# A planned two-level fast matmul kernel: sums assigned to fixed engines, a third p5 tile, zero matmuls at the start, and two products moved in the TensorE order

## Chip, cores and metric

The kernel runs on one core of one Trainium2 chip. The metric is the device time in microseconds (us); lower is better. Before the change three runs were taken, and their median is compared. Besides these, one execution was recorded by the hardware profiler; all durations of single instructions below come from that one.

## Reference

A batch of 1024 rows `x` with 512 features goes through a factorization layer with 64 embeddings:

```python
def _L0_rec_ref(x, weight, lin_w, lin_b):
    out_lin = x @ lin_w.T + lin_b
    xv = jnp.einsum('bf,efm->bem', x, weight)
    zp = jnp.einsum('bf,efm->bem', jnp.square(x), jnp.square(weight))
    interaction = 0.5 * jnp.sum(jnp.square(xv) - zp, axis=1)
    return out_lin + interaction
```

`x` is 1024 x 512, `weight` 64 x 512 x 512, `lin_w` 512 x 512, all in float32. There are three parts: `lin`, one matmul with a bias; `xv`, the large one, a 1024 x 512 by 512 x 32768 matmul whose result is only squared and summed over the embeddings; and `zp`, which needs just one small matmul, because the squared weights can be summed over the embeddings first.

## The kernel before, in words

**Tiling.** The columns of `weight` are cut into 16 groups of 2048 columns (32 output columns times 64 embeddings). For each group the kernel multiplies a 2 x 2 block matrix of x by a 2 x 2 block matrix of weights (`w11`, `w12`, `w21`, `w22`, 1 MB each) by a fast scheme with seven products in place of eight. It does so at two levels. Each of the seven outer products is called a *tree*; trees run in the order `ORDER = (1, 6, 2, 7, 5, 4, 3)`. Within a tree seven inner products are made, and `PLACE` gives each its place in the order of TensorE: product p of tree number s has the key `7 * s + PLACE[p]`. Products of up to three neighbouring trees alternate, so product 5 of a tree comes before the end of the tree before it. A product is two calls of matmul of 128 x 128 by 128 x 512 in float32, which the profile shows as four instructions. The trees are 3136 of the 3264 matmul instructions.

**Operands of a tree.** The x side (`X1` to `X7`) is made once at the start: two copies and sums of 1024 elements per partition on block level, then four sums of 256 elements per `X` (L280, and L372 for the form -a - b). The weight side is made for every tree: four sums `t1` to `t4` of 128 x 512 on GpSimd (L280), out of one weight tile, with two tiles for each. Trees 5 and 6 use `T1` and `T2`, sums of weight blocks that are built by a plain load (L309) and accumulating loads issued by GpSimd (L413). `w12` and `w21` get an accumulation of this kind later in the group.

**Results of a tree.** Products accumulate in PSUM banks `b1`, `b3` and the ring `b2`. `p5` and `p53` are copies of `b3` in SBUF, after product 5 and after product 3. Where the key word in the code is `early`, `p5` is a sum with an addend (`oa3` or `ob3`) made on VectorE; otherwise ScalarE copies it (L293). Outer results are kept in `oa0` to `oa3` and `ob0` to `ob3` and in the ring `c`. For tree 5 and the positions 1 and 3 the code does

```python
o = c_ring()
whole(p, b, p, psum=True)
whole(o, f"oa{pos}", p)
whole(f"ob{pos}", f"ob{pos}", p)
```

so `p` is read by two SBUF sums, `c` and `ob`. A finished result is squared on ScalarE (L295) and reduced on VectorE into `acc` (L302). Squares of the weights go the same way into `w2_sum`.

**Order of work.** Nothing is ordered by hand: each operation is given to a `Plan` with its cost on each engine that could do it, its reads and its writes. `Plan.order` works out the latest time of each from the TensorE chain, then simulates the engines and emits the instructions in the order that came out. Each engine, and each queue that issues transfers, then runs its own instructions strictly in that order. `HOP` is the time that the plan takes for a signal between engines. An operation with costs for VectorE and GpSimd could go to either. VectorE took one only when its latest time was under `spare` = 4 us away. For operations marked `both`, the plan also counted what the two engines lose when they run at once.

**Start and end.** Lin comes first: 64 matmul instructions (L331) on four banks, for which x and `lin_w` are loaded in quarters (k = 0 to 3) into `oa0` to `oa3`, `ob0`, `ob1`. Its bias is added on VectorE into `ob2`, `ob3`, `c_0`, `c_1`, and the sums are stored in DRAM (`lind`). At the end zp comes as 64 matmul instructions (L617) on the same banks, with x squared on VectorE beforehand (L588); the parts of `acc` are joined with lin (L598), zp is added (L280), and eight stores follow.

Of the kernel before, what the change touches and what calls it, by code (L numbers as in the profile page):

```python
# [11 lines left out]
F32 = mybir.dt.float32  # L12
# [4 lines left out]
P = 128  # L17
# [9 lines left out]
class Plan:  # L27
# [5 lines left out]

    HOP = 0.18

    def __init__(self):
        self.ops = []
# [19 lines left out]
        op.deps.discard(op.n)  # L59
        self.ops.append(op)  # L60

    def order(self, spare=4.0):
        ops = self.ops
        chain = sorted((o for o in ops if o.key is not None), key=lambda o: o.key)
        t = 0.0
        for o in chain:
            o.latest = t
            t += o.costs[PE]
        for o in reversed(ops):
            for d in o.deps:  # L70
                ops[d].succ.append(o.n)
        waiting = [len(o.succ) for o in ops]
        stack = [o for o in ops if not o.succ]
        while stack:
            o = stack.pop()
            latest = t if o.latest is None else o.latest
            cost = min(o.costs.values()) + o.land + self.HOP
            for x in o.succ:
                latest = min(latest, ops[x].latest - cost)
            o.latest = latest  # L80
            for d in o.deps:
                waiting[d] -= 1
                if not waiting[d]:
                    stack.append(ops[d])

        left = [len(o.deps) for o in ops]
        pending = {e: set() for e in (PE, ACT, DVE, POOL, SP)}
        free = dict.fromkeys(pending, 0.0)
        running = dict.fromkeys(pending)
        times = [self.HOP]  # L90
        done, late, nxt = [], 0.0, 0

        def release(o):
            for e in o.costs:
                pending[e].add(o.n)

        def ready(o):
            return max([0.0] + [ops[d].end for d in o.deps]) + self.HOP

        def longer(e, by):  # L100

            free[e] += by
            running[e].end += by
            heapq.heappush(times, free[e])
            heapq.heappush(times, running[e].end + self.HOP)

        for o in ops:
            if not left[o.n]:
                release(o)

        def pick(e, now):
            if e == PE:
                if nxt < len(chain):
                    o = chain[nxt]
                    if not left[o.n] and ready(o) <= now + 1e-6:
                        return o
                return None
            at = {n: ready(ops[n]) for n in pending[e]}
            for n in sorted((n for n in at if at[n] <= now + 1e-6),
                            key=lambda n: (ops[n].latest, n)):  # L120
                o = ops[n]
                if len(o.costs) > 1 and e == DVE and o.latest + late - now > spare:
                    continue
                until = now + o.costs[e]
                if not any(
                    now + 1e-6 < at[u] < until - 0.2
                    and ops[u].latest < o.latest
                    and ops[u].latest + late < until + 0.1
                    for u in at
                ):  # L130
                    return o
            return None

        while len(done) < len(ops):
            now = heapq.heappop(times)
            moved = True
            while moved:
                moved = False
                for e in pending:
                    if free[e] > now + 1e-6:  # L140
                        continue
                    o = pick(e, now)
                    if o is None:
                        continue
                    moved = True
                    if e == PE:
                        nxt += 1
                        late = max(late, now - o.latest)
                    cost = o.costs[e]

                    if e == DVE and o.both and free[POOL] > now + 0.1:
                        over = free[POOL] - now
                        cost += 0.9 * over
                        longer(POOL, 0.35 * over)
                    elif e == POOL and free[DVE] > now + 0.1 and running[DVE].both:
                        over = free[DVE] - now
                        cost += 0.5 * over
                        longer(DVE, 0.9 * over)
                    free[e] = now + cost
                    running[e] = o  # L160
                    o.end = free[e] + o.land
                    heapq.heappush(times, free[e])
                    heapq.heappush(times, o.end + self.HOP)
                    for f in o.costs:
                        pending[f].discard(o.n)
                    done.append((o, e))
                    for x in o.succ:
                        left[x] -= 1
                        if not left[x]:
                            release(ops[x])  # L170
        return done
# [3 lines left out]
def kernel(  # L175
# [34 lines left out]
    nc = tc.nc  # L210
# [43 lines left out]
        make(f"oa{pos}", half)  # L254
        make(f"ob{pos}", half)
    t_ring = {k: ring(f"t{k}", 2, [P, N]) for k in range(1, 5)}
    p5_ring, p53_ring = ring("p5", 2, half), ring("p53", 3, half)
    c_ring, wsq_ring = ring("c", 3, half), ring("wsq", 2, half)
    make("b1", [P, G, N], ps)
    make("b3", [P, G, N], ps)  # L260
    b2_ring = ring("b2", 2, [P, G, N], ps)
    acc_ring = ring("acc", 2, [P, NB, MG])
    w2_sum = sb.tile([P, NK, M], F32, tag="w2_sum", name="w2_sum")
    bias = sb.tile([P, M], F32, tag="bias", name="bias_sb")
    acc_dram = dram.tile([P, NB, M], F32, tag="accd", name="accd")
    lin_dram = dram.tile([P, NB, M], F32, tag="lind", name="lind")

# [1 line left out]
    engines = {DVE: nc.vector, POOL: nc.gpsimd}  # L269
    PAIR = 1.72  # L270

    def two_input(o, a, b, sub, size=1024, psum=False):

        costs = {DVE: 0.08 + 1.06 * size / 1024}
        if not psum:
            costs[POOL] = 0.14 + 2.19 * size / 1024

        def emit(e):
            f = engines[e].tensor_sub if sub else engines[e].tensor_add
            f(o, a, b)  # L280

        return costs, emit

    def whole(o, a, b, sub=False, only=None, psum=False):

        costs, emit = two_input(buf[o], buf[a], buf[b], sub, psum=psum)
        plan.add({e: c for e, c in costs.items() if only in (None, e)}, emit, (a, b), (o,),
                 both=not psum)

    def act(o, i, func, reads, writes, cost=1.04):  # L290
        def emit(_):
# [19 lines left out]

    x_src = xT.rearrange("(p k) b -> p k b", k=NK)
    lw_src = lin_wT.rearrange("(p k) m -> p k m", k=NK)
    nc.gpsimd.dma_start(bias, lin_b.partition_broadcast(P))
    for k in range(NK):
        q, r = divmod(k, KH)
        for h in range(2):
            name = f"oa{2 * h + q}"
            dma(buf[name][:, r, :], x_src[:, k, ts(h, H)], (), ((name, r),),
                1.2, 2.0, nc.sync if h == 0 else nc.scalar)  # L320
        dma(buf[f"ob{q}"][:, r, :], lw_src[:, k, :], (), ((f"ob{q}", r),), 1.2, 2.0)

    lin_banks = ["b1", "b3", "b2_0", "b2_1"]
    for k in range(NK):
        q, r = divmod(k, KH)
        for g, bank in enumerate(lin_banks):
            h = g // 2

            def emit(_, k=k, q=q, r=r, g=g, h=h, bank=bank):
                for j in range(G):  # L330
# [6 lines left out]
                    )  # L337

            plan.add({PE: PAIR}, emit, ((f"oa{2 * h + q}", r), (f"ob{q}", r)),
                     (bank,), key=-1000 + 4 * k + g)  # L340
    for g, bank in enumerate(lin_banks):
        o = ("ob2", "ob3", "c_0", "c_1")[g]
        for j in range(G):
            costs, emit = two_input(buf[o][:, j, :], buf[bank][:, j, :], bias, False, 512, True)
            plan.add(costs, emit, (bank,), ((o, j),))
        dma(lin_dram[:, ts(g, G), :], buf[o], ((o, 0), (o, 1)), (o,))

    def block4(i):
# [15 lines left out]
    def x_sum(i, o, a, b, kind, reads, size):  # L364

        if kind != "-a - b":
            costs, emit = two_input(o, a, b, kind == "a - b", size)
        else:
            costs = {DVE: two_input(o, a, b, True, size)[0][DVE]}

            def emit(_):
                nc.vector.scalar_tensor_tensor(o, a, -1.0, b, ALU.mult, ALU.subtract)  # L372
# [77 lines left out]
    def tree(s, g, i):  # L450
# [3 lines left out]
        for k, a, b, reads in (  # L454
# [2 lines left out]
            (3, b22, b12, (r,)),  # L457
            (4, b21, buf[t[2]], (r, t[2])),
        ):
            costs, emit = two_input(buf[t[k]], a, b, True, 512)  # L460
            plan.add({POOL: costs[POOL]}, emit, reads, (t[k],))
        rhs = {
            1: (b11, r), 2: (b21, r), 3: (b22, r), 4: (buf[t[4]], t[4]),
            5: (buf[t[1]], t[1]), 6: (buf[t[2]], t[2]), 7: (buf[t[3]], t[3]),
# [142 lines left out]
        add_acc(g, edge, M, buf[last][:, ts(g, G), :], reads)  # L607

    out_dst = out.rearrange("(n p) m -> p n m", p=P)
    w2_parts = tuple(("w2", row, m * MI) for row in range(2) for m in range(M // MI))  # L610
    for g, bank in enumerate(("b3", "b1", "b2_0", "b2_1")):
        o = acc_all[g]
        h = g // 2
        for j in range(G):
            def emit(_, bank=bank, g=g, h=h, j=j):
                for k in range(NK):
# [5 lines left out]
                    )  # L622

            plan.add({PE: 2 * PAIR}, emit, (xe[h, 0], xe[h, 1]) + w2_parts,
                     ((bank, j),) + ((bank,) if j == 0 else ()), key=1e6 + 2 * g + j)
            costs, emit = two_input(
                buf[o][:, j, :], buf[bank][:, j, :], buf[lin_all[g]][:, j, :], False, 512, True
            )
            plan.add(costs, emit, ((bank, j), lin_all[g], o), ((o, "out", j),))
            dma(out_dst[:, g * G + j, :], buf[o][:, j, :], ((o, "out", j),), ())  # L630
# [35 lines left out]
```

## Time and profile before

| | |
|---|---|
| device time, median of 3 | 1430.11 us (1429.66 to 1430.48) |
| device time of the profiled run | 1429.27 us |
| span of the profile, first to last instruction | 1427.5 us |
| TensorE matmul | 1409.1 us busy, 3264 instructions |
| VectorE | 1115.5 us busy, 946 instructions |
| GpSimd (POOL) | 1010.6 us busy, 703 instructions |
| ScalarE | 678.8 us busy, 692 instructions |
| moved by DMA | 200.96 MB, mean 141 GB/s; 269 GB/s in the first 10 us, 376 and 344 in the two after |

In the profile's lines, PE is TensorE's matmul and PEld its weight load, DVE is VectorE, ACT ScalarE, POOL GpSimd, SP the engine that issues most transfers. A timeline line gives start, duration (both in us), engine, line of the code, operation and operands (out<-in, the numbers of buffers left out), and in brackets the idle time just before and what ended it. Matmul ends are modelled, so the distance from one start to the next says more than the duration.

### The profile page before, as it was taken

How to read it: one execution, taken by the hardware profiler on the slowest of the kernel's cores; microseconds unless marked ns; L12 is line 12 of the kernel's file. 1: busy time of each engine (PE TensorE's matmuls, PEld its weight loads, DVE VectorE, ACT ScalarE, POOL GpSimd, SP SyncE). 2: the span in 40 equal slices, each digit the busy share in tenths (PEclk: the TensorE clock that was granted, in tenths of full speed). 3: DMA queues.
4: the chain of work that ended last, by engine and by line, in shares of the span. 5: the costliest groups of instructions: out<-in, count | busy, mean ns of one | idle time of the engine just before them, and what ended most of it. 6: DMA issues, size and time to landing. Idle time of an engine off the chain costs nothing.

```text
span 1427.5 us, 10368 instructions
## 1 busy us (share of the span) xinstructions
PE 1409.1 (99%) x3264; PEld 617.9 (43%) x3264; DVE 1115.5 (78%) x946; ACT 678.8 (48%) x692; POOL 1010.6 (71%) x703
## 2 busy tenths in 40 slices
PE   8999999999999999999999999999999999999998
PEld 3434444444444444444444444444444444444443
DVE  1779597886968779696877959788696978969785
ACT  1446354454635446364544635445463544636431
POOL 5886786857768686785958678685777868677660
PEclk9999999999999999999999999999999999999999
DMA  9656381745628175472836638274573817546331
GB/s 306 202 155 173 91 203 45 196 122 143 167 75 205 67 177 151 118 177 63 209 89 164 163 96 199 55 193 113 147 177 91 187 53 185 143 120 145 94 112 60
DMA packets 47286, 200.96 MB, mean 141 GB/s; under 512 B 19008, under 2 KB 20032, under 8 KB 24704
## 3 DMA queue, kind: packets, MB, share of 16 engines
q0 software_dynamic: 11600, 84.15, 30.2%
q1 hardware_dynamic: 35056, 115.09, 23.3%
q10 hardware_dynamic: 576, 1.05, 0.2%
q8 instruction: 27, 0.44, 0.1%
q14 instruction: 27, 0.22, 0.0%
HBM read 177.34 MB, written 6.16 MB: 129 GB/s over the span
## 4 chain that ended last, share of the span: by engine, by line
PE 92%; DMA 2%; POOL 2%; DVE 2%; issue 1%; ACT 0%; DVEq 0%; SPq 0%; ACTq 0%; POOLq 0%
PE b L472 90%; DMA T<-weight 2%; PE b L617 2%; DVE p L280 1%; POOL t L280 1%; POOL X L280 1%; DMA oa<-xT 0%; POOL ob L280 0%; DVE ob L280 0%; ACT X L293 0%; SPq L309 0%; POOL w L413 0%; DVE w22a L280 0%; DVEq L662 0%; ACTq L309 0%
## 5 line engine op out<-in xcount | busy, mean ns | idle before, releaser
L472 PE MATMUL b<-t,X 128*128 128x512 f32 x1792 | 806.1, 592 | 1.7 <-DVE ob L280 1.4
L472 PEld LDWEIGHTS b<-t,X 128*128 128x128 f32 x1792 | 339.2, 190 | 432.1 <-issue 419.9
L472 PE MATMUL b<-w,X 128*128 128x512 f32 x768 | 358.5, 592 | 3.4 <-DVE p L280 2.3
L280 POOL TENSOR_TENSOR t<-w 128x512 f32<-128x512 f32 x128 | 163.2, 1278 | 147.5 <-PE b L472 84.5
L472 PEld LDWEIGHTS b<-w,X 128*128 128x128 f32 x768 | 145.7, 190 | 187.8 <-issue 175.1
L293 ACT COPY p<-b 128x1024 f32<-128x1024 f32 x160 | 160.4, 1002 | 133.6 <-PE b L472 133.6
L295 ACT ACTIVATE oa<-oa 128x1024 f32<-128x1024 f32 x128 | 133.6, 1056 | 166.8 <-DVE oa L280 166.8
L280 POOL TENSOR_TENSOR t<-w,t 128x512 f32<-128x512 f32 x128 | 164.9, 1289 | 57.5 <-PE b L472 57.3
L472 PE MATMUL b<-T,X 128*128 128x512 f32 x384 | 180.4, 592 | 0.0
L302 DVE TENSOR_REDUCE acc<-oa 128x16 f32<-128x1024 f32 x128 | 152.1, 1208 | 18.0 <-ACT oa L295 18.0
L302 DVE TENSOR_REDUCE w_sum<-wsq 128x16 f32<-128x1024 f32 x128 | 152.8, 1204 | 0.2 <-ACT wsq L295 0.2
L293 ACT COPY b<-b 128x1024 f32<-128x1024 f32 x112 | 112.4, 1004 | 82.2 <-PE b L472 82.2
L280 DVE TENSOR_TENSOR oa<-b,p 128x1024 f32<-128x1024 f32 x96 | 116.6, 1214 | 34.7 <-PE b L472 34.7
L295 ACT ACTIVATE wsq<-w 128x1024 f32<-128x1024 f32 x96 | 98.0, 1054 | 70.0 <-DVE w_sum L302 66.5
L280 POOL TENSOR_TENSOR t<-T 128x512 f32<-128x512 f32 x64 | 83.5, 1305 | 47.5 <-issue 33.2
L295 ACT ACTIVATE c<-c 128x1024 f32<-128x1024 f32 x64 | 65.8, 1055 | 106.7 <-DVE c L280 102.8
L472 PEld LDWEIGHTS b<-T,X 128*128 128x128 f32 x384 | 73.0, 190 | 91.8 <-issue 88.2
L280 DVE TENSOR_TENSOR p<-b,p 128x1024 f32<-128x1024 f32 x80 | 97.3, 1216 | 17.9 <-PE b L472 17.9
L280 DVE TENSOR_TENSOR ob<-b,p 128x1024 f32<-128x1024 f32 x48 | 58.5, 1218 | 65.0 <-PE b L472 65.0
L295 ACT ACTIVATE ob<-ob 128x1024 f32<-128x1024 f32 x64 | 67.6, 1058 | 87.3 <-DVE ob L280 87.3
L280 DVE TENSOR_TENSOR oa<-b,oa 128x1024 f32<-128x1024 f32 x64 | 77.8, 1216 | 29.8 <-PE b L472 29.8
L280 POOL TENSOR_TENSOR t<-T,t 128x512 f32<-128x512 f32 x64 | 82.0, 1281 | 25.5 <-PE b L472 25.5
(55 smaller groups left out, 1328.4 us busy)
## 6 DMA issues: line engine op xcount, KB each, us to landing
w<-weight SPq DMA_DIRECT2D x48, 1024.0 KB, 4.9
T<-weight POOLq DMA_DIRECT2D x48, 1024.0 KB, 8.2
T<-weight SPq DMA_DIRECT2D x32, 1024.0 KB, 4.8
w<-weight POOLq DMA_DIRECT2D x16, 1024.0 KB, 10.8
w<-T POOLq DMA_DIRECT2D x16, 1024.0 KB, 6.9
w22a<-weight SPq DMA_DIRECT2D x8, 1024.0 KB, 6.1
w22b<-weight SPq DMA_DIRECT2D x8, 1024.0 KB, 5.9
w<-xT SPq DMA_DIRECT2D x4, 512.0 KB, 4.7
```

What stands on the lines that cost most here:

```text
L280: f(o, a, b)
L293: nc.scalar.copy(o, i)
L295: nc.scalar.activation(o, i, func)
L302: lambda _: nc.vector.tensor_reduce(o, i.rearrange("p a (m e) -> p a m e", e=E), axis=AX.X, op=ALU.add),
L472: nc.tensor.matmul(buf[b][:, j, :], buf[f"X{i}"][:, SLOT[p], ts(j, P)], op, start=first, stop=True, skip_group_check=True,)
L617: nc.tensor.matmul(buf[bank][:, j, :], buf[xe[h, k // KH]][:, k % KH, ts((g * G + j) % (NB // 2), P)], w2_sum[:, k, :], start=(k == 0), st ...
```

## The change

- SBUF sums no longer have two candidate engines. A sum of two SBUF tiles that `whole` makes (with `psum` false) is always GpSimd's; sums that read PSUM and all sums of the x side are always VectorE's. The rule with `spare` in `pick` is gone, and `HOP` is 0.3 instead of 0.18.
- `p5` has three tiles instead of two. The bias has no tile of its own any more and uses the second tile of `t4` until that is needed.
- The loads of x and `lin_w` are issued ahead of the plan: eight x loads on SP, four `lin_w` loads on ScalarE's queue. The plan keeps only the time at which each is taken to have landed (4.0 + 2.5 k us).
- VectorE clears a tile, and TensorE does three matmuls on these zeros into `b1` and `b3` ahead of lin.
- Lin takes the banks in the order `b3`, `b1`, `b2_0`, `b2_1`. Its last product (k = 3, bank `b2_1`) goes behind product 5 of the first tree.
- The first half of zp's first bank goes ahead of the last product of the last tree; the other seven halves follow the last product, as before.

```diff
@@ -33,7 +33,7 @@
 
 
 
-    HOP = 0.18
+    HOP = 0.3
 
     def __init__(self):
         self.ops = []
@@ -59,7 +59,7 @@
         op.deps.discard(op.n)
         self.ops.append(op)
 
-    def order(self, spare=4.0):
+    def order(self):
         ops = self.ops
         chain = sorted((o for o in ops if o.key is not None), key=lambda o: o.key)
         t = 0.0
@@ -119,8 +119,6 @@
             for n in sorted((n for n in at if at[n] <= now + 1e-6),
                             key=lambda n: (ops[n].latest, n)):
                 o = ops[n]
-                if len(o.costs) > 1 and e == DVE and o.latest + late - now > spare:
-                    continue
                 until = now + o.costs[e]
                 if not any(
                     now + 1e-6 < at[u] < until - 0.2
@@ -254,14 +252,14 @@
         make(f"oa{pos}", half)
         make(f"ob{pos}", half)
     t_ring = {k: ring(f"t{k}", 2, [P, N]) for k in range(1, 5)}
-    p5_ring, p53_ring = ring("p5", 2, half), ring("p53", 3, half)
+    p5_ring, p53_ring = ring("p5", 3, half), ring("p53", 3, half)
     c_ring, wsq_ring = ring("c", 3, half), ring("wsq", 2, half)
     make("b1", [P, G, N], ps)
     make("b3", [P, G, N], ps)
     b2_ring = ring("b2", 2, [P, G, N], ps)
     acc_ring = ring("acc", 2, [P, NB, MG])
     w2_sum = sb.tile([P, NK, M], F32, tag="w2_sum", name="w2_sum")
-    bias = sb.tile([P, M], F32, tag="bias", name="bias_sb")
+    bias = buf["t4_1"]
     acc_dram = dram.tile([P, NB, M], F32, tag="accd", name="accd")
     lin_dram = dram.tile([P, NB, M], F32, tag="lind", name="lind")
 
@@ -269,23 +267,20 @@
     engines = {DVE: nc.vector, POOL: nc.gpsimd}
     PAIR = 1.72
 
-    def two_input(o, a, b, sub, size=1024, psum=False):
-
-        costs = {DVE: 0.08 + 1.06 * size / 1024}
-        if not psum:
-            costs[POOL] = 0.14 + 2.19 * size / 1024
+    def two_input(engine, o, a, b, sub, size=1024):
+
+        costs = {DVE: 0.08 + 1.06 * size / 1024, POOL: 0.14 + 2.19 * size / 1024}
 
         def emit(e):
             f = engines[e].tensor_sub if sub else engines[e].tensor_add
             f(o, a, b)
 
-        return costs, emit
-
-    def whole(o, a, b, sub=False, only=None, psum=False):
-
-        costs, emit = two_input(buf[o], buf[a], buf[b], sub, psum=psum)
-        plan.add({e: c for e, c in costs.items() if only in (None, e)}, emit, (a, b), (o,),
-                 both=not psum)
+        return {engine: costs[engine]}, emit
+
+    def whole(o, a, b, psum=False):
+
+        costs, emit = two_input(DVE if psum else POOL, buf[o], buf[a], buf[b], False)
+        plan.add(costs, emit, (a, b), (o,))
 
     def act(o, i, func, reads, writes, cost=1.04):
         def emit(_):
@@ -311,20 +306,34 @@
 
     x_src = xT.rearrange("(p k) b -> p k b", k=NK)
     lw_src = lin_wT.rearrange("(p k) m -> p k m", k=NK)
-    nc.gpsimd.dma_start(bias, lin_b.partition_broadcast(P))
+    def landing(name, at):
+        plan.add({SP: 0.0}, None, (), (name,), land=at)
+
     for k in range(NK):
         q, r = divmod(k, KH)
-        for h in range(2):
-            name = f"oa{2 * h + q}"
-            dma(buf[name][:, r, :], x_src[:, k, ts(h, H)], (), ((name, r),),
-                1.2, 2.0, nc.sync if h == 0 else nc.scalar)
-        dma(buf[f"ob{q}"][:, r, :], lw_src[:, k, :], (), ((f"ob{q}", r),), 1.2, 2.0)
-
-    lin_banks = ["b1", "b3", "b2_0", "b2_1"]
+        x0, x1, l = f"oa{q}", f"oa{2 + q}", f"ob{q}"
+        nc.sync.dma_start(buf[x0][:, r, :], x_src[:, k, ts(0, H)])
+        nc.scalar.dma_start(buf[l][:, r, :], lw_src[:, k, :])
+        nc.sync.dma_start(buf[x1][:, r, :], x_src[:, k, ts(1, H)])
+        for name in (x0, l, x1):
+            landing((name, r), 4.0 + 2.5 * k)
+    nc.gpsimd.dma_start(bias, lin_b.partition_broadcast(P))
+
+
+    zero = buf["t1_0"]
+    nc.vector.memset(zero, 0.0)
+    for j in range(3):
+        nc.tensor.matmul(
+            buf[("b1", "b3")[j // 2]][:, j % 2, :], zero[:, 0:P], zero, start=True, stop=True
+        )
+    plan.add({PE: 4.0}, None, (), ("b1", "b3"), key=-2000)
+
+    lin_banks = ["b3", "b1", "b2_0", "b2_1"]
     for k in range(NK):
         q, r = divmod(k, KH)
         for g, bank in enumerate(lin_banks):
             h = g // 2
+            late = k == NK - 1 and g == 3
 
             def emit(_, k=k, q=q, r=r, g=g, h=h, bank=bank):
                 for j in range(G):
@@ -337,12 +346,12 @@
                     )
 
             plan.add({PE: PAIR}, emit, ((f"oa{2 * h + q}", r), (f"ob{q}", r)),
-                     (bank,), key=-1000 + 4 * k + g)
+                     (bank,), key=PLACE[5] + 0.5 if late else -1000 + 4 * k + g)
     for g, bank in enumerate(lin_banks):
         o = ("ob2", "ob3", "c_0", "c_1")[g]
         for j in range(G):
-            costs, emit = two_input(buf[o][:, j, :], buf[bank][:, j, :], bias, False, 512, True)
-            plan.add(costs, emit, (bank,), ((o, j),))
+            costs, emit = two_input(DVE, buf[o][:, j, :], buf[bank][:, j, :], bias, False, 512)
+            plan.add(costs, emit, (bank, "t4_1"), ((o, j),))
         dma(lin_dram[:, ts(g, G), :], buf[o], ((o, 0), (o, 1)), (o,))
 
     def block4(i):
@@ -364,9 +373,9 @@
     def x_sum(i, o, a, b, kind, reads, size):
 
         if kind != "-a - b":
-            costs, emit = two_input(o, a, b, kind == "a - b", size)
+            costs, emit = two_input(DVE, o, a, b, kind == "a - b", size)
         else:
-            costs = {DVE: two_input(o, a, b, True, size)[0][DVE]}
+            costs = two_input(DVE, o, a, b, True, size)[0]
 
             def emit(_):
                 nc.vector.scalar_tensor_tensor(o, a, -1.0, b, ALU.mult, ALU.subtract)
@@ -457,8 +466,8 @@
             (3, b22, b12, (r,)),
             (4, b21, buf[t[2]], (r, t[2])),
         ):
-            costs, emit = two_input(buf[t[k]], a, b, True, 512)
-            plan.add({POOL: costs[POOL]}, emit, reads, (t[k],))
+            costs, emit = two_input(POOL, buf[t[k]], a, b, True, 512)
+            plan.add(costs, emit, reads, (t[k],))
         rhs = {
             1: (b11, r), 2: (b21, r), 3: (b22, r), 4: (buf[t[4]], t[4]),
             5: (buf[t[1]], t[1]), 6: (buf[t[2]], t[2]), 7: (buf[t[3]], t[3]),
@@ -607,6 +616,7 @@
         add_acc(g, edge, M, buf[last][:, ts(g, G), :], reads)
 
     out_dst = out.rearrange("(n p) m -> p n m", p=P)
+    last_key = 7 * (7 * NG - 1) + PLACE[4]
     w2_parts = tuple(("w2", row, m * MI) for row in range(2) for m in range(M // MI))
     for g, bank in enumerate(("b3", "b1", "b2_0", "b2_1")):
         o = acc_all[g]
@@ -622,9 +632,10 @@
                     )
 
             plan.add({PE: 2 * PAIR}, emit, (xe[h, 0], xe[h, 1]) + w2_parts,
-                     ((bank, j),) + ((bank,) if j == 0 else ()), key=1e6 + 2 * g + j)
+                     ((bank, j),) + ((bank,) if j == 0 else ()), 
+                     key=last_key - 0.5 if (g, j) == (0, 0) else last_key + 1 + 2 * g + j)
             costs, emit = two_input(
-                buf[o][:, j, :], buf[bank][:, j, :], buf[lin_all[g]][:, j, :], False, 512, True
+                DVE, buf[o][:, j, :], buf[bank][:, j, :], buf[lin_all[g]][:, j, :], False, 512
             )
             plan.add(costs, emit, ((bank, j), lin_all[g], o), ((o, "out", j),))
             dma(out_dst[:, g * G + j, :], buf[o][:, j, :], ((o, "out", j),), ())
```

## Prediction

> **What bounds the kernel now.** I read the page first: TensorE is busy 1409.1 of 1427.5 us, the other engines 78% at most. So only TensorE's own idle time counts. Next the waits of TensorE alone (engine, waited for: us in total, times, longest):
>
> ```profile
> PE b L331 <- DMA ob<-lin_wT: 6.0, 1, 6.0
> PE b L472 <- DVE p L280: 5.3, 17, 2.3
> PE b L472 <- DVE ob L280: 1.4, 1, 1.4
> PE b L472 <- ACT p L293: 1.1, 1, 1.1
> ```
>
> These are 13.8 us. Then the timeline, because a busy TensorE can be a slow one. The first weight loads of lin (start, duration):
>
> ```profile
> 10.36 0.34 PEld L331 LDWEIGHTS b<-ob,oa 128*128 128x128 f32 x1 [0.52 <-issue]
> 11.21 0.34 PEld L331 LDWEIGHTS b<-ob,oa 128*128 128x128 f32 x1 [0.52 <-issue]
> 11.93 0.19 PEld L331 LDWEIGHTS b<-ob,oa 128*128 128x128 f32 x1 [0.38 <-DMA ob<-lin_wT]
> 12.36 0.19 PEld L331 LDWEIGHTS b<-ob,oa 128*128 128x128 f32 x1 [0.24 <-issue]
> ```
>
> Until 11.2 us a matmul comes every 0.855 us, afterwards every 0.429 us (ten steps from 15.79 to 20.08). Lin's 64 instructions start at 5.96 and the trees at 36.39: 30.43 us instead of 64 x 0.4292 = 27.47, so 2.96 us are lost to a slow start.
>
> In the middle TensorE waits 15 times, 0.2 us each, once a group. One case, the three views TensorE, VectorE, GpSimd:
>
> ```profile
> 1208.89 1.88 PE L472 MATMUL b<-w,X 128*128 128x512 f32 x4
> 1210.93 1.98 PE L472 MATMUL b<-w22b,X 128*128 128x512 f32 x4 [0.17 <-DVE p L280]
> 1212.75 1.88 PE L472 MATMUL b<-t,X 128*128 128x512 f32 x4
> ```
>
> ```profile
> 1202.80 1.21 DVE L280 TENSOR_TENSOR p<-b,p 128x1024 f32<-128x1024 f32 x1
> ...
> 1205.06 3.56 DVE L280 TENSOR_TENSOR c<-oa,p 128x1024 f32<-128x1024 f32 x1
> 1208.54 1.21 DVE L302 TENSOR_REDUCE w_sum<-wsq 128x16 f32<-128x1024 f32 x1
> 1209.67 1.21 DVE L280 TENSOR_TENSOR p<-b,ob 128x1024 f32<-128x1024 f32 x1
> ```
>
> ```profile
> 1204.92 2.61 POOL L280 TENSOR_TENSOR ob<-ob,p 128x1024 f32<-128x1024 f32 x1
> 1207.48 2.27 POOL L280 TENSOR_TENSOR t<-w22b,t 128x512 f32<-128x512 f32 x1
> ```
>
> A product of four matmuls takes 1.717 us. Here the starts are 2.04 and 1.82 us apart: 0.32 + 0.10 = 0.43 us lost, more than the 0.17 shown, since the weight loads no longer run ahead. Product 3 of tree 3 waits for p5 (1209.67), which needs ob3 (ready at 1207.53) and sits behind the sum c = oa3 + p5, 3.56 us on VectorE. The same tile p5 is also read by that c: with two tiles, tree 3 gets the one that tree 5 used. The last group has the other placement, GpSimd taking c:
>
> ```profile
> 1374.38 3.33 POOL L280 TENSOR_TENSOR c<-oa,p 128x1024 f32<-128x1024 f32 x1
> ```
>
> There products start at 1378.02 and 1379.74, with no wait. The other losses, by the same subtraction: first tree (36.39 to 42.91) 1.37; 70.38 to 78.63, three products in 8.25 us, 3.1; before the last product:
>
> ```profile
> 1390.13 1.88 PE L472 MATMUL b<-t,X 128*128 128x512 f32 x4
> 1393.42 1.95 PE L472 MATMUL b<-t,X 128*128 128x512 f32 x4 [1.41 <-DVE ob L280]
> ```
>
> 1.57 + 0.07 = 1.64. The span: 5.96 first load + 2.96 slow start + 3264 x 0.4292 = 1400.9 + 1.37 + 3.1 + 15 x 0.43 = 6.45 + 1.64 + 4.66 after the last matmul (1422.84) = 1427.0 of 1427.5. Nearly everything is named.
>
> **What the Trainium skill says.** "TensorE: Matmul & The Clock Gate", Part 1: the array is half rate until it was busy for a window of about 3.4 us, and the window runs free of the kernel, so the moment varies. The trace agrees on the factor (0.855 to 0.429); the rise came some 5.5 us after the first matmul, within one to two windows. "SBUF — State Buffer", Who interferes with whom: a VectorE instruction with two SBUF inputs contends with a GpSimd instruction that reads SBUF; with one such input it doesn't. The trace agrees: c on VectorE takes 3.56 us where sums with a PSUM input take 1.21, and GpSimd's t took 2.27 beside it against 1.27.
>
> **The change part by part.** Sums are made against the profiled span, 1427.5; that run took 1429.27 us and the three others 1429.66 to 1430.48, so I take the difference off their median 1430.11.
>
> *Zero matmuls.* Three matmuls are six instructions: 6 x 0.855 = 5.1 us, the memset before them is not in the trace; nearest is a 128x512 add from PSUM, 0.68. SP and ACT issue at 0.75, so memset to 1.45, zeros 1.5 to 6.6. Lin's first data were there at 5.96, so the zeros hold it back 0.6 us. The clock rises 3.4 to 6.8 us after 1.5, i.e. by 4.9 to 8.3; what is still slow after 6.6 loses half: 0 to 0.85, I take 0.4. Lin's start counts as 7.0 instead of 5.96 + 2.96 = 8.92: gain 1.9. Bounds: 3.2 (zeros end at 5.7 as the clock rises among them) and -0.6 (zeros don't warm it and only delay).
>
> *Loads.* SP issued four x and four lin_w loads, ACT four x; now eight x go on SP and four lin_w on ACT, all ahead of any weight load on these queues. The bias stays GpSimd's first issue. 3.25 MB at some 0.35 MB/us (343 to 376 GB/s here) from 2 us on are in by 11.3 us, and lin needs its second quarter only at 7.0 + 6.9 = 13.9: TensorE hides them. But T2's first load, issued at 2.60 and landed after 8.3 us at 10.9, now lands near 14.2. Its two accumulating loads (12.7 and 9.5 us in the trace) were issued at 12.83, held up by GpSimd's X sums, and 25.81. Now: 14.3 + 12.7 + 0.3 + 9.5 = 36.8, and with one t sum 38.1. TensorE needs that t after 60 lin instructions and four products, at 7.0 + 25.75 + 6.9 = 39.6: hidden with 1.5 us to spare, or less if more weight loads run beside it.
>
> *Lin's last product behind tree 0's product 5.* Nothing is added; it gives ACT 1.72 us for its copy of p5 (1.01 us): gain 1.37, bounds 0 and 1.37. Lin's last two bias adds (0.68 each) and their store move 1.7 us back, beside products. The bias in t4's second tile binds only tree 1's t4, used by product 4 some 27 us into the trees: hidden.
>
> *Sums by engine.* X sums leave GpSimd: 24 small x 0.77 (18.5) and two large of 2.63, 23.8 us, all in the first 70. VectorE takes them in its first 31 us, where it has nothing to do. The stall near 75 is a chain on GpSimd: a t sum waits for T1 until 62.34, then ob sums to 73.2, then VectorE's p. I expect two thirds gone: 2.1 of 3.1, bounds 3.1 and -2, as T1's arrival (15.5 us for one load under contention) is not set by GpSimd.
>
> In each group c goes from VectorE (3.58 mean x 15) to GpSimd (2.36, bounds 2.35 to 3.33). GpSimd's 1010.6 us lose 23.8 and gain 16 x 2.4 = 38: 72% of the span, no bound on average. Behind c on GpSimd: two t sums (7 to 10 us ahead of their products), a weight accumulate and oa<-p,oa. ob3 is due four products before c's own reader is, so it should go first and end by 1207.3. VectorE is then free, and with the third p5 tile p5 needn't await c: it can end at 1208.6, due 1210.4. Gain 15 x 0.43 = 6.4. Bounds: 6.4, and a loss by the first rival.
>
> *One zp product ahead of the last tree product.* It is 8 x 0.43 = 3.4 us of work set into the wait of 1.57. Its inputs are ready (x squares end at 1368.6, b3 is copied by 1383.2). Its own sum and store still wait for the last reduces at 1407; the tail of 4.66 us stays. Gain 1.6, bounds 0 and 1.64.
>
> *HOP and the dropped spare rule* alter only the order. No row prices this: 0, with 1 us either way.
>
> Sum: 1.9 + 1.4 + 2.1 + 6.4 + 1.6 = 13.4; 1430.1 - 13.4 = 1416.7. All waits gone would be 15.8, and about 1414.
>
> **The rivals.** *GpSimd comes too late in tree 5 (slower).* If it takes c before ob3: 1204.95 + 2.36 + 2.36 = 1209.7, p5 ends at 1211.0, a wait of 0.5 + 0.25 for refilling = 0.75, hardly worse than 0.43. With a further t sum (1.27) ahead, 2.0 a group: 15 x (2.0 - 0.43) = 24 less the 7.0 won at both ends, +17: 1447. It decides once ob3 ends over 2.3 us later than its 1207.5. For it: GpSimd is the engine that gains work, in its densest tree (three sums and two t in 11 us already). Against: the last group, where GpSimd had c without a wait. 0.11.
>
> *T2 or T1 is late (faster, less).* Loads now stand behind 3.25 MB; DMA shares are at 1.0 from 2 to 34 us. 3.5 us beyond the slack, plus the old stall kept (2.1): 1416.7 + 5.6 = 1422, span of the case 1420 to 1426. For it: the slack of 1.5 us. 0.15.
>
> *The group's wait stays.* VectorE's reduces, not c, would hold p5; then 6.4 are lost: 1423. Against: the reduce is only 1.21 of the 4.77 us ahead of p5. 0.08.
>
> *The zeros don't do what they say* (clock not raised, 2.5 us less): 1419, inside the main range. No change at all needs new waits of 10 to 16 us: 0.05.
>
> **How the numbers follow.** The main case, 1413.5 to 1420, has 0.61; with the second and third rivals 0.84 is faster, of which I leave 0.01 to a loss elsewhere: 0.83 faster, 0.05 same, 0.12 slower. 0.2% is 2.9 us, about what a measurement here can tell. The range 1413.5 to 1426 holds these first three cases, a little over 8 in 10; its low end is the case of no waits.
>
> **What would show it.** Right: lin's weight loads 0.43 us apart from about 7 us; no TensorE wait for ACT p near 38 or for DVE ob near the end; c on GpSimd at 2.4 us, no two-SBUF sum on VectorE after the start; group period 84.1 instead of 84.55. Wrong: TensorE waits for POOL t near 39, or waits longer than 0.2 us once a group for p; a span above 1424.

## The result and the profile after

The changed kernel takes 1419.4 us (median of 6 runs, 1419.27 to 1420.8) against 1429.41 us (6 runs) for the kernel before; the ratio is 0.9933, 95% interval 0.9921 to 0.9946. That is 10.0 us less; 1416.7 was predicted, within 1413.5 to 1426. The span of the profiled run is 1418.9 us, 8.6 less than before. That run took 1420.72 us, as TensorE's clock fell in it for a while (shown below); four of the six runs are at 1419.3 to 1419.5.

TensorE's waits in the changed kernel (engine, waited for: us in total, times, longest):

```profile
PE b L481 <- DVE oa L276: 2.9, 3, 2.4
PE b L326 <- DVE t L324: 1.5, 1, 1.5
PE b L481 <- DVE ob L276: 1.2, 1, 1.2
```

The 17 waits for `p` are gone, and so is the one for ScalarE's `p`; L326 is the zero matmuls waiting for their tile. A wait for `oa` is new. All stages can be compared by one number: the distance between the starts of TensorE's weight loads, less 0.4292 us for each.

| lost, us | before | after | gain | predicted |
|---|---|---|---|---|
| first weight load of lin | 5.92 | 5.51 | 0.41 | |
| slow clock in lin | 2.57 | 0 | 2.57 | 1.9 for both |
| first tree | 1.37 | 1.39 | 0.0 | 1.4 |
| later in the first group | 3.10 | 4.30 | -1.2 | 2.1 |
| 15 groups | 6.62 | 0 | 6.6 | 6.4 |
| last group | 1.73 | 1.64 | 0.1 | 1.6 |

The gains add up to 8.5 us, near the 8.6 us between the two spans. So the predicted range and the largest term held. The sum was too high, 13.4 us against 10.0: three of the smaller terms gave nothing or less, and the start gave more than its term, for another reason than was predicted.

The number for lin's slow clock is that of one profile. In the profiles of the experiments below that keep the zeros, lin lost between 0 and 1.0 us to it.

**Start.** Weight loads (start, duration): the last of the zeros, then lin.

```profile
4.18 0.34 PEld L326 LDWEIGHTS b<-t 128*128 128x128 f32 x1 [0.52 <-issue]
5.04 0.23 PEld L326 LDWEIGHTS b<-t 128*128 128x128 f32 x1 [0.52 <-issue]
5.51 0.19 PEld L340 LDWEIGHTS b<-ob,oa 128*128 128x128 f32 x1 [0.24 <-issue]
5.94 0.19 PEld L340 LDWEIGHTS b<-ob,oa 128*128 128x128 f32 x1 [0.24 <-issue]
```

The step of 0.855 us ends among the zeros, some 3.6 us after their start; in this profile all of lin runs at 0.43.

**A group.** The place that cost 0.43 us in every group, in the views of TensorE, VectorE and GpSimd:

```profile
1201.32 1.88 PE L481 MATMUL b<-w,X 128*128 128x512 f32 x4
1203.03 1.88 PE L481 MATMUL b<-w22b,X 128*128 128x512 f32 x4
```

```profile
1200.25 1.21 DVE L276 TENSOR_TENSOR p<-b,ob 128x1024 f32<-128x1024 f32 x1
```

```profile
1197.35 2.62 POOL L276 TENSOR_TENSOR ob<-ob,p 128x1024 f32<-128x1024 f32 x1
1199.67 2.62 POOL L276 TENSOR_TENSOR c<-oa,p 128x1024 f32<-128x1024 f32 x1
```

The product on `w22b` follows after 1.71 us, without a wait. `ob` comes ahead of `c` on GpSimd, and `p` starts at 1200.25, while `c` still runs until 1202.3 on the other tile.

**First group.** VectorE; then TensorE's two waits, the second as weight loads:

```profile
28.65 1.22 DVE L297 TENSOR_REDUCE w_sum<-wsq 128x16 f32<-128x1024 f32 x1 [9.19 <-ACT wsq L290]
...
31.58 1.28 DVE L276 TENSOR_TENSOR ob<-b,t 128x512 f32<-128x512 f32 x2
...
39.29 8.87 DVE L276 TENSOR_TENSOR X<-X 128x256 f32<-128x256 f32 x8
48.08 1.21 DVE L276 TENSOR_TENSOR oa<-b,p 128x1024 f32<-128x1024 f32 x1
```

```profile
33.01 1.96 PE L481 MATMUL b<-t,X 128*128 128x512 f32 x4 [1.16 <-DVE ob L276]
```

```profile
49.35 0.41 PEld L481 LDWEIGHTS b<-t,X 128*128 128x128 f32 x2 [3.20 <-DVE oa L276]
50.27 0.34 PEld L481 LDWEIGHTS b<-t,X 128*128 128x128 f32 x1 [0.52 <-issue]
51.13 0.34 PEld L481 LDWEIGHTS b<-t,X 128*128 128x128 f32 x1 [0.52 <-issue]
```

VectorE stands still for 9.19 us behind a reduce of squares of `w12`, which landed only at 27.5 us. The two bias sums of bank `b3` (`ob`, at 31.58) come behind that reduce and one more, and the first tree's product 5 waits for them. The X sums queued behind the first reduce then run beside GpSimd's t sums, 1.1 us each, where eight of them took 2.76 us together near 11 us. `oa` is late, TensorE waits 2.4 us, and its clock drops: steps of 0.855 us again until 52.84. The wait of 2.4 us costs 4.3.

**Last group.** One of VectorE's joins of acc with lin, and `c` of tree 5 on GpSimd:

```profile
1367.44 2.17 DVE L607 SCALAR_TENSOR_TENSOR T<-w22a,T 128x960 f32<-128x960 f32 x1
```

```profile
1368.56 3.28 POOL L276 TENSOR_TENSOR c<-oa,p 128x1024 f32<-128x1024 f32 x1
```

The two overlap. Both have two SBUF inputs, and both are slower than alone (1.14 us for a join at 1377.45, and 2.36 for `c`). Tree 3's operands come late, and TensorE loses 1.64 us between 1372 and 1383, ahead of the place that zp's product was to fill.

### The profile page after: what moved, and what is told of

Same layout as the page of the kernel before. It is cut to its first block, busy times and chain, and to the rows that moved or that the text cites. A ratio compares the mean times of both kernels' runs of the same rounds, so it can differ in the third digit from the quotient of the medians.

```text
span 1418.9 us, 10383 instructions
## 1 busy us (share of the span) xinstructions
PE 1408.6 (99%) x3270; PEld 621.9 (44%) x3270; DVE 1082.0 (76%) x957; ACT 681.8 (48%) x692; POOL 1014.1 (71%) x693
## 3 DMA queue, kind: packets, MB, share of 16 engines
q10 hardware_dynamic: 576, 1.05, 0.2%
## 4 chain that ended last, share of the span: by engine, by line
PE 95%; DMA 2%; DVE 2%; POOL 1%; issue 0%; ACT 0%; ACTq 0%; DVEq 0%; SPq 0%
PE b L481 93%; PE b L627 2%; DMA w<-weight 1%; DVE X L276 1%; DMA ob<-lin_wT 1%; POOL ob L276 0%; POOL c L276 0%; DVE w_sum L297 0%; DVE c L276 0%; DVE ob L276 0%; POOL oa L276 0%; ACT oa L290 0%; ACTq L316 0%; POOL t L276 0%; DVE p L276 0%
## 5 line engine op out<-in xcount | busy, mean ns | idle before, releaser
L276 POOL TENSOR_TENSOR t<-w 128x512 f32<-128x512 f32 x128 | 171.2, 1337 | 147.6 <-PE b L481 91.8
L276 POOL TENSOR_TENSOR t<-T,t 128x512 f32<-128x512 f32 x64 | 86.4, 1350 | 18.1 <-PE b L481 18.1
L276 DVE TENSOR_TENSOR p<-b,oa 128x1024 f32<-128x1024 f32 x32 | 39.2, 1224 | 65.6 <-PE b L481 65.6
```

## Experiments

All start from the changed kernel unless another is named; times are medians, to be held against 1419.4, and the ratio with its interval is to the kernel before, run on the same chip. The runs were made on several chips, where the kernel before had medians of 1428.4 to 1429.4 us, so the times alone don't tell differences of about 1 us.

**The engine of c and the third tile: two by two.** `p5_two`:

```diff
-    p5_ring, p53_ring = ring("p5", 3, half), ring("p53", 3, half)
+    p5_ring, p53_ring = ring("p5", 2, half), ring("p53", 3, half)
```

> The changed kernel with two p5 tiles instead of three. Theory A (the third tile is needed once GpSimd makes c): p5 of tree 3 must wait until GpSimd has made both ob3 and c of tree 5, which in the changed kernel's trace is at 1202.3 us, while p5 starts at 1200.25; a TensorE wait of 0.8 to 2 us comes back in every group, 12 to 29 us over 15 groups: 1431 to 1448. Theory B (the engine of c alone removed the group's wait): 1419.4, no TensorE wait between 100 and 1350 us.

`c3_vector`:

```diff
-                whole(o, f"oa{pos}", p)
+                whole(o, f"oa{pos}", p, dve=pos == 3)
```

Here `dve` makes `whole` choose VectorE.

> The changed kernel, three p5 tiles, but the sum c = oa3 + p5 of tree 5 on VectorE, as it was before. Theory A (the 3.6 us that this sum blocks VectorE for is what made TensorE wait): a wait of about 0.2 us, 0.43 us lost, comes back in each group: 6.5 us, 1426. Theory B (the third tile alone frees p5, which then goes ahead of c): 1419.4.

`c3_vector_p5_two` has both edits.

> The changed kernel with both undone: c of position 3 on VectorE and two p5 tiles. Either theory expects the old wait of each group, 15 x 0.43 = 6.5 us: 1426. If it is at 1419.4, neither was the cause and the plan's other settings were.

| us | c on GpSimd | c on VectorE |
|---|---|---|
| three p5 tiles | 1419.4 | 1433.53, 1.0024 (1.0017 to 1.0032) |
| two p5 tiles | 1433.53, 1.0028 (1.0017 to 1.0040) | 1432.68, 1.0025 (1.0015 to 1.0035) |

Neither half alone does anything; together they take 13 to 14 us off, more than the 6.6 us that they brought against the kernel before, whose order was made with other settings. With two tiles and c on GpSimd, in the views of GpSimd, VectorE and TensorE:

```profile
1293.29 2.63 POOL L276 TENSOR_TENSOR c<-oa,p 128x1024 f32<-128x1024 f32 x1
1295.61 2.64 POOL L276 TENSOR_TENSOR ob<-ob,p 128x1024 f32<-128x1024 f32 x1
```

```profile
1298.45 1.22 DVE L276 TENSOR_TENSOR p<-b,ob 128x1024 f32<-128x1024 f32 x1
```

```profile
1299.72 1.98 PE L481 MATMUL b<-w22a,X 128*128 128x512 f32 x4 [0.58 <-DVE p L276]
```

The plan put `c` ahead of `ob`. With two tiles both must be done before the tile is free, so by its code the plan gives them one latest time and takes the first in line. `p` follows the second by 0.2 us, and TensorE loses 0.85 us a group, the lower end of theory A (1431). With c on VectorE and three tiles the plan still put c there ahead of `p`:

```profile
1208.48 3.06 DVE L276 TENSOR_TENSOR c<-oa,p 128x1024 f32<-128x1024 f32 x1
1211.47 1.21 DVE L297 TENSOR_REDUCE w_sum<-wsq 128x16 f32<-128x1024 f32 x1
1212.60 1.21 DVE L276 TENSOR_TENSOR p<-b,ob 128x1024 f32<-128x1024 f32 x1
```

This loses the old 0.44 us a group, as theory A had it, and a second 0.35 us near the next tree that it didn't have: VectorE has no pause from 1205 to 1233, and the backlog reaches a further product. The corner with both edits loses the same two amounts (0.43 and 0.35). So both corners with c on VectorE are 7 us slower than expected, and the 0.35, which the kernel before doesn't lose, comes from the other settings of the changed plan; these were not taken apart.

**The zeros.** `no_zeros` leaves out the memset and the three matmuls:

```diff
-    nc.vector.memset(zero, 0.0)
-    for j in range(3):
-        nc.tensor.matmul(
...
```

> The changed kernel without the memset and the three matmuls on zeros; the plan and every order stay as they are. My theory (the zeros only raise TensorE's clock ahead of lin): lin's first seven or so weight loads are 0.855 us apart again instead of 0.429, which costs 2.6 to 3.0 us, so about 1422.2 us against 1419.4. Rival (the early start comes from the new order of the loads, the zeros add nothing): 1419.4 within 0.5 us, or below it as lin can start some tenths earlier.

1419.41 us (five runs, 1416.9 to 1420.94), 0.9930 (0.9917 to 0.9944): the time is as the rival had it. The first weight loads of lin without zeros:

```profile
4.94 0.50 PEld L335 LDWEIGHTS b<-ob,oa 128*128 128x128 f32 x2 [4.94 <-DMA ob<-lin_wT]
...
7.66 0.30 PEld L335 LDWEIGHTS b<-ob,oa 128*128 128x128 f32 x1 [0.52 <-issue]
8.20 0.19 PEld L335 LDWEIGHTS b<-ob,oa 128*128 128x128 f32 x1 [0.24 <-issue]
```

Lin starts 0.57 us earlier and loses 1.11 us to the slow clock, so its last weight load ahead of product 5 (31.38 instead of 30.83) is 0.55 us later. That is all that the zeros win between these two profiles, and it is no more than chance gives: in `join_late` and `zp_last` below, which have the zeros, the same load comes at 31.41 and 31.82, because the clock rose later. The wait for VectorE's bias sum near 32 takes most of the 0.55 back: 1.39 us lost there with zeros, 1.02 without. This profile, of a run of 1419.27 us, also has the wait for `oa` (2.3 us) without a drop of the clock: 2.70 us lost there instead of 4.30.

`no_zeros_old_queues` also puts the loads on the queues of before:

```diff
-        nc.scalar.dma_start(buf[l][:, r, :], lw_src[:, k, :])
-        nc.sync.dma_start(buf[x1][:, r, :], x_src[:, k, ts(1, H)])
+        nc.sync.dma_start(buf[l][:, r, :], lw_src[:, k, :])
+        nc.scalar.dma_start(buf[x1][:, r, :], x_src[:, k, ts(1, H)])
```

> The changed kernel without zeros and with the loads of x and lin_w on the queues that the kernel before had (lin_w and half of x on SP in turn, the other half of x on ScalarE's queue), still ahead of everything else. Theory A (without zeros lin starts at 4.9 us and not at 5.96 as lin_w went out at once on a queue of its own): lin's first matmul goes back to about 5.9 us, the time is 1 us above that without zeros, 1420.4. Theory B (the start is set by something else, such as the bias load or the memory's first answer): first matmul at 4.9 us, 1419.4.

1421.46 us, 0.9945 (0.9933 to 0.9958), 2.05 above `no_zeros`. Lin's first matmul comes at 8.22 us, waiting for `lin_w`, later than theory A said. In this run four x loads on ScalarE's queue are out by 2.6 us beside it, where the kernel before had issued one by then; that this is the reason was not tested. Lin starts 3.3 us later and loses 1.5 us more to the slow clock (2.58), and the two waits behind it, shorter by 2.6 (none near 32, 1.10 us lost near 50), give that much back.

`before_again` is the kernel before once more, for its profile alone.

> The kernel before once more, for a second look at its start. If the slow start is a matter of chance (when the clock rises after TensorE begins), its first weight loads are 0.855 us apart for another number of steps than seven; the waits of 0.2 us in each group are the same as in the first profile.

1428.42 us. The last full step of 0.855 us ended 4.4 us after the first weight load (5.3 in the first profile), with 1.94 us lost instead of 2.57; the 15 waits cost 0.40 to 0.46 us each as before.

**Lin's late product.** `lin_plain`:

```diff
-                     (bank,), key=PLACE[5] + 0.5 if late else -1000 + 4 * k + g)
+                     (bank,), key=-1000 + 4 * k + g)
```

> The changed kernel with lin's last product in its old place, ahead of product 5 of the first tree. Theory A (as predicted, the move hides ScalarE's copy of p5): 1.4 us slower, 1420.8. Theory B (in the changed kernel product 5 waits for VectorE's bias sums of bank b3 anyway, and with lin's last product in front it would not wait): within 0.5 us of 1419.4, the wait for DVE ob gone and one for ACT p in its place.

1424.02 us, 0.9966 (0.9953 to 0.9978): 4.6 slower than the changed kernel, so neither theory. TensorE waits twice for ScalarE's `p` (1.9 us together), and the first tree loses 2.36 us instead of 1.39: the move is worth 1.0 us there. The rest comes from the new order behind it: ten X sums and two reduces now run on VectorE between 39 us and `oa`, where the changed kernel has eight X sums, TensorE waits 4.2 us for it, its clock drops, and 6.79 us are lost instead of 4.30.

**X sums behind a reduce.** `squares_late` gives the plan a landing for the squares alone:

```diff
+            if g == 0 and q != "w22":
+                plan.add({SP: 0.0}, None, (n,), ((n, "in"),), land=8.0)
+                reads = (n, (n, "in"))
```

> The changed kernel, but the plan takes the squares of the first group's w11, w12 and w21 to be possible 8 us later than it did, so that VectorE's queue has nearly all X sums ahead of the first w_sum reduce. Theory A (the loss near 47 us comes from X sums that stand behind that reduce, which waits for w12 until 28.6 us, and then run beside GpSimd's t sums at 1.1 us instead of 0.35): VectorE's idle 9 us go, TensorE's waits for DVE ob at 32 and DVE oa at 47 go, 3 to 5.5 us faster: 1414 to 1416.5. Theory B (the late arrival of T2 and w21 bounds this stretch): the wait changes its name, to POOL t or DMA, and the time stays at 1419.4 within 1 us.

1416.69 us (1416.26 to 1416.9), 0.9915 (0.9901 to 0.9928), the fastest version: theory A for these waits. VectorE's X sums and TensorE's first wait in its list:

```profile
18.19 4.44 DVE L276 TENSOR_TENSOR X<-X 128x256 f32<-128x256 f32 x13
```

```profile
PE b L485 <- POOL t L276: 1.9, 1, 1.9
```

Thirteen X sums now run at 18 us at 0.34 us each, and the waits for `ob` at 32 and `oa` at 47 are gone. Theory B is right in part: a new wait of 1.9 us for GpSimd's t, 2.2 lost, stands at 38 us, because T2's last load lands at 38.9. GpSimd works beside these X sums too:

```profile
17.99 6.98 POOL L276 TENSOR_TENSOR t<-w 128x512 f32<-128x512 f32 x2 [1.50 <-DMA w<-weight]
```

Here its two t sums are the slow ones, 3.49 us each where 1.27 is usual, and the X sums keep their 0.34. In the changed kernel near 40 us it was the other way round. In both places the overlap cost one of the two engines time; what decides which was not tested.

**The last group.** `zp_last` puts zp's first half back behind the last tree product:

```diff
-                     key=last_key - 0.5 if (g, j) == (0, 0) else last_key + 1 + 2 * g + j)
+                     key=last_key + 1 + 2 * g + j)
```

> The changed kernel with the first half of zp's first bank behind the last tree product again. Theory A (that half hides a real wait of the last product): product 7 ends near 1384.9 us and VectorE delivers ob3 only at 1387.7, since a join with acc stands in front of it; the last product waits 2.8 us, 1422.2 against 1419.4. Theory B (the wait only moved from there to tree 3, where 1.64 us are lost in the changed kernel, so the move itself is worth nothing): 1419.4 within 0.7.

1422.16 us, 0.9956 (0.9943 to 0.9970): the time of theory A to the tenth, but in part by luck. TensorE in the last group:

```profile
1377.71 3.70 PE L481 MATMUL b<-t,X 128*128 128x512 f32 x8 [1.88 <-DVE oa L276]
1386.29 1.96 PE L481 MATMUL b<-t,X 128*128 128x512 f32 x4 [1.44 <-DVE ob L276]
```

The last product waits 1.44 us and not 2.8, and 1.67 us are lost there, about the 1.64 of the kernel before. So in the changed kernel the move does hide a wait, of the predicted size. The stretch from 1371 on loses 4.06 us instead of 1.64; the rest of these 2.4 us stands in tree 3, where 2.39 us are lost instead of 1.64, as the plan's order there changed with the move.

`join_late` makes the joins wait for the last product's results:

```diff
-        add_acc(g, 0, edge, buf[acc_all[g]][:, :, 0:edge], (acc_all[g],))
+        add_acc(g, 0, edge, buf[acc_all[g]][:, :, 0:edge], (acc_all[g], (last, 3, 3)))
```

> The changed kernel, but the four sums that join acc with lin (960 elements, two SBUF inputs) wait for the last product's results, so they leave tree 5 of the last group. Theory A (these sums and GpSimd's sums of tree 5 hold each other up, 2.17 us instead of 1.1 and 3.3 instead of 2.36, and so delay p and oa): the 1.64 us lost between 1372 and 1383 go, the joins fit behind the zp matmuls: 1417.8. Theory B (GpSimd alone has too much in the last tree 5, with the squares of x beside it): 1.64 us stay, 1419.4, or later by up to 2 us if the joins delay the last stores.

The trace gives theory A in most: c takes 2.38 us on GpSimd at 1367.86, and 0.59 us are lost instead of 1.64. The time, 1419.91 us (1418.03 to 1420.14), 0.9936 (0.9923 to 0.9948), can't tell: the profiled run has the drop of the clock near 50 us, and by their times three of the other four seem to have it too.

**HOP.** `hop_018` has `HOP = 0.18`.

> The changed kernel with HOP at 0.18 as before. Theory A (HOP only shifts orders, priced at nothing): 1419.4 within 1 us, no wait that returns in each group. Theory B (with the shorter signal time the plan puts instructions too early and a wait returns in each group): a wait of 0.2 us or more, 15 times, 3 us or more slower.

1419.69 us, 0.9934 (0.9920 to 0.9947): no wait returns in the groups, theory A.

**Together.** `best` is `squares_late` with the joins of `join_late` and

```diff
-        outer_sum(g, 1)
+        outer_sum(g, 1, ("T2",) if g == 0 else ())
```

so that T1's accumulating load reads T2 for the plan and waits for it.

> The kernel of squares_late with two more edits: the accumulating load of T1 in the first group waits until T2 is complete, and the joins of acc with lin are late as in join_late. Theory A (T2's last load lands at 38.9 us because T1's load, issued 2.3 us after it, shares the DMA engines with it; its wait of 1.9 us costs 2.2): T2 is there 2 us or more earlier, the wait for POOL t goes, and with the 1 us of the joins the time is 1413.5. Theory B (T2 is late because of its first two loads and w22, not of T1): the wait for POOL t stays, 1415.7.

1418.68 us, 0.9920 (0.9907 to 0.9934), no better than `squares_late`: the medians are 2.0 us apart, of which 1.0 is also between the kernels before on the two chips. The last group's loss is 0.58 us, but T2 comes still later; its first t sum on GpSimd:

```profile
40.20 2.48 POOL L276 TENSOR_TENSOR t<-T 128x512 f32<-128x512 f32 x2 [11.18 <-DMA T<-weight]
```

The wait for t stays, as theory B had it. But the plan also moved a load of `w22b` forward to 12.43 us, so another 1 MB ran beside T2. Whether T1's load holds T2 up is therefore not decided, and what bounds T2 is not settled. The wait grew to 2.8 us and the clock dropped after it.

## Why the prediction was right, and where it was not

*The groups, 6.4 predicted, 6.6 measured.* The mechanism was that c holds VectorE and p5's tile; the run of `ob` ahead of `c`, the start of `p` before c's end and the wait of zero are as described. The two by two shows what the prediction only argued: engine and tile are both needed. What one alone would have done in the old plan is not shown, as each run has its own order. The slower rival had GpSimd taking c first; in these profiles that happened only with two tiles. HOP was tested alone and is worth nothing that shows; moving the X sums and dropping the spare rule were not.

*Start, 1.9 predicted, 2.98 in the profile.* The failed step is the cause: the prediction put the gain down to the zeros. Of the 2.98 us, 0.98 come from the loads: lin's first weight load is at 4.94 in `no_zeros` and was at 5.92. Before, `lin_w` was second on SP; now it is first on its own queue, which the prediction didn't count. `no_zeros_old_queues` shows that the queues matter here, but not why it starts as late as 8.2. The zeros give 0.55, no more than chance gives. The other 1.46 us lie between the 2.57 that the kernel before lost to the slow clock and the 1.11 of `no_zeros`, which has no zeros either. The prediction took this loss as fixed (2.96, or 2.57 by weight loads), but the same kernel lost 1.94 in its second look: it depends on when the clock rises. "TensorE: Matmul & The Clock Gate" of the Trainium skill says as much in Part 1: the window runs free of the kernel. The half microsecond either way that it gives in one place is too little for these runs, where the last slow step ended 2.7 to 5.3 us after the first weight load.

*First tree, 1.4 predicted, 0.* The wait for ScalarE's copy went, as said. The step "Lin's last two bias adds (0.68 each) and their store move 1.7 us back, beside products" overlooked the first two: those of b3 gate product 5, and they stood behind the reduce at 28.65. `lin_plain` loses 2.36 us there, so the move itself was worth 1.0.

*Stall of the first group, 2.1 predicted, -1.2.* "VectorE takes them in its first 31 us, where it has nothing to do" failed. VectorE had the time, but not the order: the reduce that waited for `w12` stood ahead of the X sums. `squares_late`, which moves only the squares in the plan, shows that this order was the cost. Why the plan expected `w12` early is read from its code and was not tested: it takes the x loads to cost SP nothing (`{SP: 0.0}`). The wait for T2 at 38.9 us that remains in `squares_late` is the second rival's, predicted at 36.8 for the landing; in the changed kernel the earlier waits of TensorE hid it.

*Last product, 1.6 predicted, 0.1.* The fill works: without it 1.67 us are lost ahead of the last product (`zp_last`). But the term left out that VectorE's joins and GpSimd's tree 5 would meet in the last group: GpSimd now has all sums there. `join_late` takes 1.05 of the 1.64 us away in the trace.

One sum of the prediction is slightly off: the upper bounds of its five terms add up to 15.7, where it says that all waits gone would be 15.8. Nothing rests on it.

## What to carry to other kernels

When one consumer holds both a slow engine and a buffer, a change to either alone may show nothing; test the pair. When work moves to an idle engine, check not only its free time but what will stand in front of it in that engine's order, and when that thing's data really land. Where TensorE is 99% busy, compare the distances between weight loads: they show a slow clock and the refill after a wait, which a list of waits leaves out.

## What was not expected of the hardware

TensorE's clock rose at different moments: the last full step of 0.855 us ended 2.7 us after the first weight load in `no_zeros` and 5.3 us after it in `zp_last`, in the kernel before 5.3 and 4.4. It fell again after single waits of 2.2 to 2.8 us (three or four loads 0.855 us apart, the granted clock 0.91 in the mean from 36 to 56 us), but not in every run: after 2.3 us in `no_zeros` and 2.7 us in `zp_last` it stayed at 1.00. So nearly the same wait cost 4.30 us in the changed kernel's profile and 2.70 in that of `no_zeros`. What decides it was not found. These 1.6 us are about the distance between the two levels of the changed kernel's times, 1419.3 and 1420.8.
